# A transformer block with table-coded weights: look-ups twice as wide, down's first weights parked in DRAM, and the last weights copied one unit earlier

## The chip, the core and the metric

One core of a Trainium2 chip runs the kernel in one launch. The metric is the device time of that launch in microseconds (us), as the median of several runs. A separate execution was recorded by the hardware profiler; all views of the profile come from that one execution. Engines are named as in the profile: PE (TensorE, matmuls), PEld (its weight loads), DVE (VectorE), ACT (ScalarE), POOL (GpSimd, which here only issues DMAs), SP (SyncE, which only issues DMAs). "L783" is line 783 of the kernel.

## The reference

The block is attention across the embedding axis, and then a gated feed-forward layer whose weights are 4-bit indices into a table of 16 numbers:

```python
x = x + attn(_layernorm(x), Wq, Wk, Wv, Wo)     # x: 2 x 2048 x 512, float32
w = lut[idx]                                    # lut: 16 numbers; idx: int32, 0 to 15
gate = einsum('bsh,oh->bso', y, lut[gate_idx])  # y = _layernorm(x); gate_idx: 1376 x 512
up   = einsum('bsh,oh->bso', y, lut[up_idx])    # up_idx: 1376 x 512
h    = silu(gate) * up
x    = x + einsum('bso,ho->bsh', h, lut[down_idx])   # down_idx: 512 x 1376
```

## The kernel before, in words

**Stages.** The 4096 rows are taken as 8 chunks c of 512 rows, four blocks j of 128 in each. First come the Gram matrices of the normalised rows (`gram`, L458), then products of 512 x 512 matrices in Strassen's manner (`square`, L662) with the softmax among them, then y, the attention's result (`y_product`, L779), and the second norm. Then follow the gate/up units (`GateUp`, L1013), the rows of the last 96 hidden columns (`LastRows`, L1232) and the down product in 32 units (`Down`, L1413).

**Blocks of hidden columns.** 1376 is 10 blocks f of 128 and one of 96 (`NFT` = 11). A gate/up unit (f, p) makes block f for the pair p of chunks. All products are Strassen products: sums of operands are made on DVE, products are added up in PSUM, and parts are copied out by ACT or added by DVE. From f = 2 on two units are joined into a second level; such a unit has a role: 0 and 1 for even f (p even, odd), 2 and 3 for odd f. Units of role 3 are short.

**Order.** Each engine's instructions run in the order in which the program writes them, and the order is written by hand. A unit runs in stages (`Line.run`, L1179), and after each stage `between` (L1311) is called. It may write a load, some waiting sums, or a little of the look-ups: `pump(us)` (L407) adds `us` to an account and calls `step` (L398) until the account is used up. `step` writes the next piece of work, whose cost in the planner's microseconds is what the generator yields. `pace` sets how much a stage gives: 0.85, 1.4, 1.0 and 0.6 for roles 0 to 3.

**Look-ups.** `looked_up` (L381) runs through `jobs` (L376). A job (`Job`, L246) turns up to 128 x 512 indices into weights. `fetch` loads them from DRAM by POOL's queue, `cast` makes 16-bit copies on ACT (L259), and `ops` writes 19 DVE instructions: three masks (L271, L272, L277), the lowest bit spread into a mask (L275), and a tree of eight selections between two table entries ("leaves", L285) with seven predicated copies (L297). The eighth leaf is the 16th of the 19 instructions, and three copies follow it. Gate and up of a block are two jobs; each of down's 11 blocks is one. Index tiles have two buffers: job i + 2 is fetched when job i has been written, and job i + 1 is cast in the middle of job i. A job's `gate` keeps it from starting before its destination is free: `passed` and `ended` count the f whose last unit has been written, or has had its fourth a-product written in the following unit.

**Weights.** Gate weights lie in `wg` and up weights in `wu`, three buffers each. The sums of both (`of_both`, L345) are put off until an older f has ended. Down's first six blocks stay in SBUF from their look-up to the end, in `wd` (L119, 12 KB of each partition); the others are looked up during the down product, into `wd2`.

**The end of the units.** After the last unit (9, 3) the program writes what is left of the look-ups, opens new pools, asks SP for three loads of h (L1371), and has ACT copy the last block's gate and up weights side by side into one tile (L1250, L1251). Then 16 groups of 16 matmuls follow (L1285), each in one of four PSUM banks in turn; ACT and DVE empty a group into `hrow`. Between the groups DVE makes further sums of the last weights and of down's first blocks (`down_sums`, L1346).

## Time and profile before

| what | value |
|---|---|
| median of 3 runs | 1066.43 us (1066.21 to 1067.09) |
| the profiled execution's own time | 1067.22 us |
| its span from first to last instruction | 1065.4 us |
| granted TensorE clock | full |
| moved by DMA | 189 MB, 177 GB/s over the span |

The span by stage (busy us of each engine in each stretch, from the span's start):

| stage | stretch | PE | DVE | ACT |
|---|---|---|---|---|
| Gram matrices | 7 to 77 | 69.4 | 57.2 | 40.1 |
| matrix products, softmax | 77 to 165 | 87.7 | 70.3 | 31.9 |
| y and second norm | 165 to 275 | 110.0 | 96.7 | 50.6 |
| units f = 0, 1 | 275 to 383 | 108.0 | 85.7 | 38.2 |
| units f = 2 to 9 | 383 to 750 | 365.7 | 313.0 | 155.5 |
| last rows | 750 to 793 | 42.3 | 18.9 | 6.5 |
| down, first half | 793 to 935 | 142.0 | 122.3 | 42.4 |
| down, second half | 935 to 1062 | 127.0 | 70.2 | 17.9 |

How to read the profile's lines. A line of the costliest groups or of instructions by line has: line, engine, operation, tiles (written<-read, buffer numbers left out), shape, count | busy us, mean ns of one | idle us of the engine before them and what ended it. A line of the waits has: who waited, for whom, us in total, times, longest. A timeline line has: start, duration, engine, line, operation, tiles, count, and in brackets the engine's idle time before. Matmuls overlap, and their ends are modelled, so lateness shows best in the steps from start to start.

### The profile page before, as it was taken

How to read it: one execution, taken by the hardware profiler on the slowest of the kernel's cores; microseconds unless marked ns; L12 is line 12 of the kernel's file. 1: busy time of each engine (PE TensorE's matmuls, PEld its weight loads, DVE VectorE, ACT ScalarE, POOL GpSimd, SP SyncE). 2: the span in 40 equal slices, each digit the busy share in tenths (PEclk: the TensorE clock that was granted, in tenths of full speed). 3: DMA queues.
4: the chain of work that ended last, by engine and by line, in shares of the span. 5: the costliest groups of instructions: out<-in, count | busy, mean ns of one | idle time of the engine just before them, and what ended most of it. 6: DMA issues, size and time to landing. Idle time of an engine off the chain costs nothing. (4 is left out here: it accounts for less than half of the span.)

```text
span 1065.4 us, 11592 instructions
## 1 busy us (share of the span) xinstructions
PE 1056.6 (99%) x3554; PEld 660.7 (62%) x3554; DVE 837.1 (79%) x1842; ACT 385.2 (36%) x741; POOL 105.7 (10%) x160
## 2 busy tenths in 40 slices
PE   8999999999999999999999999999999999999998
PEld 5668887444444444444444444444898888888887
DVE  7878778889985889899699999964549998656554
ACT  4652532455532234444443444443223222211111
POOL 0000000011110220230041032013000000000000
PEclk9999999999999999999999999999999999999999
DMA  8750314598561366795596679569436675666773
GB/s 345 236 169 11 86 28 99 119 237 222 158 178 50 128 228 197 172 220 183 185 207 198 208 174 225 178 192 195 150 114 230 198 228 177 203 192 211 222 227 119
DMA packets 127710, 189.07 MB, mean 177 GB/s; under 512 B 18832, under 2 KB 59024, under 8 KB 126752
## 3 DMA queue, kind: packets, MB, share of 16 engines
q1 hardware_dynamic: 74528, 100.17, 29.6%
q0 software_dynamic: 15776, 39.92, 17.4%
q10 hardware_dynamic: 37344, 48.24, 13.9%
q8 instruction: 28, 0.46, 0.2%
q14 instruction: 34, 0.28, 0.1%
HBM read 108.60 MB, written 79.69 MB: 177 GB/s over the span
## 5 line engine op out<-in xcount | busy, mean ns | idle before, releaser
L783 PE MATMUL y<-m,nT 128*128 128x512 f32 x256 | 110.2, 592 | 0.0
L783 PEld LDWEIGHTS y<-m,nT 128*128 128x128 f32 x256 | 48.6, 190 | 60.4 <-issue 57.4
L1008 PE MATMUL a_g<-xT_a,s 128*128 128x512 f32 x160 | 75.5, 594 | 0.0
L1008 PE MATMUL a_g<-xb,wg 128*128 128x512 f32 x160 | 75.4, 593 | 0.0
L1008 PE MATMUL c_g<-xb,wu 128*128 128x512 f32 x160 | 75.2, 592 | 0.0
L1008 PE MATMUL a_d<-dT,hs_a 128*128 128x256 f32 x288 | 72.6, 379 | 0.0
L467 PE MATMUL gp<-xn_a 128*128 128x128 f32 (+3 forms) x256 | 70.1, 434 | 1.8 <-DVE xn_a L184 1.5
L467 PEld LDWEIGHTS gp<-xn_a 128*128 128x128 f32 x256 | 43.9, 190 | 28.6 <-issue 15.1
L1008 PEld LDWEIGHTS a_d<-dT,hs_a 128*128 128x128 f32 x288 | 54.5, 189 | 7.7
L297 DVE COPY_PREDICATED wd<-b_wd,wd 128x512 f32<-128x512 int16 (+1 forms) x77 | 56.3, 732 | 1.3
L1008 PE MATMUL a_g<-xT_sq,s 128*128 128x512 f32 x120 | 56.7, 595 | 0.0
L1473 ACT COPY p_d<-a_d 128x256 f32<-128x256 f32 x32 | 11.9, 372 | 120.2 <-PE a_d L1008 120.2
L1008 PEld LDWEIGHTS a_g<-xb,wg 128*128 128x128 f32 x160 | 30.2, 190 | 39.0 <-issue 32.5
L1008 PEld LDWEIGHTS a_g<-xT_a,s 128*128 128x128 f32 x160 | 30.1, 190 | 38.9 <-issue 36.4
L1008 PEld LDWEIGHTS c_g<-xb,wu 128*128 128x128 f32 x160 | 30.4, 190 | 38.3 <-issue 38.0
L143 DVE TENSOR_TENSOR r<-r,p_d 128x256 f32<-128x256 f32 x64 | 26.9, 420 | 28.0 <-ACT p_d L1473 17.4
L285 DVE TENSOR_SCALAR wd<-idx_wd,lut_x,lut_sb 128x512 int32<-128x512 int32 (+1 forms) x88 | 45.9, 539 | 0.0
L1063 ACT COPY u<-a_g 128x512 f32<-128x512 f32 x40 | 23.4, 586 | 61.9 <-PE a_g L1008 59.5
L143 DVE TENSOR_TENSOR u<-c_g,u 128x512 f32<-128x512 f32 x40 | 27.5, 688 | 21.8 <-PE c_g L1008 15.5
L1285 PE MATMUL rows<-last,xb 128*128 128x192 f32 x256 | 41.9, 326 | 1.6 <-ACT last L1251 1.6
L1285 PEld LDWEIGHTS rows<-last,xb 128*128 128x128 f32 x256 | 41.6, 190 | 2.5 <-ACT last L1251 2.5
L143 DVE TENSOR_TENSOR r<-r,a_d 128x256 f32<-128x256 f32 x64 | 26.6, 416 | 20.9 <-PE a_d L1008 20.9
(345 smaller groups left out, 2207.1 us busy)
## 6 DMA issues: line engine op xcount, KB each, us to landing
hd<-h SPq DMA_DIRECT2D x80, 256.0 KB, 3.3
h<-hd SPq DMA_DIRECT2D x40, 512.0 KB, 5.9
nl<-nd SPq DMA_DIRECT2D x32, 256.0 KB, 5.6
xnd<-xn_f ACTq DMA_DIRECT2D x16, 512.0 KB, 5.9
fl<-xnd POOLq DMA_DIRECT2D x32, 256.0 KB, 6.7
xn_back<-xnd SPq DMA_DIRECT2D x32, 256.0 KB, 3.9
rd<-r SPq DMA_DIRECT2D x32, 256.0 KB, 3.0
r<-rd SPq DMA_DIRECT2D x32, 256.0 KB, 4.3
```

The source lines that it names most:

```text
L143: nc.vector.tensor_tensor(dest, a, b, ALU.add)
L285: vec.tensor_scalar(dest.bitcast(I32), idx, lut_x[:rows, k : k + 1], lut_i[:rows, at : at + 1], ALU.bitwise_and, ALU.bitwise_xor,)
L297: vec.copy_predicated(dest, masks[level - 1], t)
L467: nc.tensor.matmul(gp[b][i][:, i * P :], xn[:, i, j % 2, :], xn[:, i:, j % 2, :], start=c % CPB == 0 and j == 0, stop=c % CPB == CPB - 1 a ...
L783: nc.tensor.matmul(ys[k], nTs[k][:, i, :], m[:, i, :], start=(i == 0), stop=(i == KB - 1))
L1008: nc.tensor.matmul(ps, lhsT, rhs, start=first and i == 0, stop=i == len(pairs) - 1, skip_group_check=not first,)
L1063: nc.scalar.copy(self.u2, self.a)
L1285: nc.tensor.matmul(ps[:, jj, :], x[:, j * P : (j + 1) * P], w, start=i == 0, stop=i == len(pairs) - 1,)
L1473: nc.scalar.copy(p1, self.a)
```

## The change

A job now covers two tables' worth of columns: gate and up of one block together (`pair_job`), or two neighbouring blocks of down, 1024 columns in one instruction. There are 17 jobs in place of 33. There is one index tile, twice as wide; the next job is fetched right after the eighth leaf of the running one (`LEAVES` = 15) and cast after the running one's last instruction, with 0.9 of planner's cost for the cast. All planner's costs of the look-ups are new. A pair's gate is that of the former up job. Gate and up weights of a block share one tile `w` with three buffers. The first fetch, of two transfers, stays on SP; the second, formerly also on SP after the loads of x, goes to POOL.

Down's first six blocks are looked up two at a time into one staging buffer `wds`, stored by SP into `wdd` in DRAM, and loaded again by SP at the end of the units, behind the loads of h, into the rooms `sq1` (four blocks) and `a3` (two).

Before unit (9, 3) the program writes what is left of the last pair's look-up, and ACT's two copies of the last weights.

```diff
-    wd = wdp.tile([P, K1, E], F32, tag="wd", name="wd")
+    wdd = dram.tile([P, K1, E], F32, tag="wdd", name="wdd")
...
         def fetch(self, queue=nc.gpsimd):
-            self.idx = gub.tile([P, 512], I32, tag="idx", name=f"idx_{self.name}", bufs=2)[
-                : self.rows, : self.cols
-            ]
-            self.load(queue, self.idx)
+            t = gub.tile([P, 2, 512], I32, tag="idx", name=f"idx_{self.name}", bufs=1)
+            self.idx = self.part(t)
+            for i, of in enumerate(self.loads):
+                queue.dma_start(self.idx[:, i, :], of)
 
         def cast(self):
-            self.b3 = self.bits("b3", 2)
-            nc.scalar.copy(self.b3, self.idx)
+            self.b1 = self.bits("b1")
+            nc.scalar.copy(self.b1, self.idx)
...
-            vec.tensor_scalar(b1, b3, 2, None, ALU.bitwise_and)
-            vec.tensor_scalar(b2, b3, 4, None, ALU.bitwise_and)
-            yield 0.2 + 0.54 * f
+            b2, b3 = self.bits("b2"), self.bits("b3")
+            vec.tensor_scalar(b2, b1, 4, None, ALU.bitwise_and)
+            yield 0.15 + 0.24 * f
+            vec.tensor_scalar(b3, b1, 8, None, ALU.bitwise_and)
+            yield 0.15 + 0.24 * f
+            vec.tensor_scalar(b1, b1, 2, None, ALU.bitwise_and)
+            yield 0.15 + 0.24 * f
 
             vec.tensor_scalar(idx, idx, 31, 31, ALU.logical_shift_left, ALU.arith_shift_right)
-            yield 0.1 + 0.55 * f
-            vec.tensor_scalar(b3, b3, 8, None, ALU.bitwise_and)
-            yield 0.1 + 0.27 * f
+            yield 0.15 + 0.48 * f
...
-                    yield 0.2 + 0.55 * f
+                    yield 0.25 + 0.48 * f
...
                 vec.copy_predicated(dest, masks[level - 1], t)
-                yield 0.1 + 1.17 * f
+                yield 0.18 + 0.96 * f
...
+        def dest():
+            if i < K1:
+                t = wgu.tile([P, 2, E], F32, tag="wds", name=f"wd_{i}", bufs=1)
+            else:
+                t = wd2[0][:, i - K1 : i - K1 + k, :]
+            made.append(t[:rows, :k, :])
+            return made[0]
+
+        def after():
+            if i < K1:
+                nc.sync.dma_start(wdd[:, i : i + k, :], made[0])
+            yield 0.1
...
+    jobs = [pair_job(0), pair_job(1), down_job(0), down_job(2)]
+    for f in range(2, NFT - 1):
+        jobs.append(pair_job(f))
+        if f == 7:
+            jobs.append(down_job(4))
+    jobs += [pair_job(NFT - 1), *(down_job(i) for i in range(K1, NFT, 2))]
...
             if i == 0:
                 job.cast()
+                yield 0.9
             for k, cost in enumerate(job.ops()):
                 yield cost
-                if k == 9 and i + 1 < len(jobs):
-                    jobs[i + 1].cast()
-            if i + 2 < len(jobs):
-                jobs[i + 2].fetch()
+                if k == LEAVES and i + 1 < len(jobs):
+                    jobs[i + 1].fetch()
+            if i + 1 < len(jobs):
+                jobs[i + 1].cast()
+                yield 0.9
+
+    LEAVES = 15
...
-    jobs[1].fetch(nc.sync)
...
+        def copied(self):
+            f, r = NFT - 1, LAST
+            nc.scalar.copy(self.w[:, :, :r], gw[f])
+            nc.scalar.copy(self.w[:, :, r:], uw[f])
...
+        if (f, p) == (NFT - 2, NPR - 1):
+            while uw.get(NFT - 1) is None:
+                step()
+            last_rows = LastRows()
+            last_rows.copied()
         u = GateUp(f, p)
...
-    last_rows = LastRows()
+    for q, (tag, n) in enumerate((("sq1", 4), ("a3", 2))):
+        t = room(tag, f"wd_{tag}")[:, :n, :]
+        nc.sync.dma_start(t, wdd[:, 4 * q : 4 * q + n, :])
+        wd1 += [t[:, i, :] for i in range(n)]
```

More of the change, by code (lines that the diff above doesn't have):

```diff
@@ L109, in tile_attn_ffn @@
     small = ctx.enter_context(tc.tile_pool(name="small", bufs=3))
-    wdp = ctx.enter_context(tc.tile_pool(name="wdp", bufs=1))
     dram = ctx.enter_context(tc.tile_pool(name="dram", bufs=1, space=DRAM))
@@ L246, in tile_attn_ffn, with __init__, part @@
     class Job:
-        def __init__(self, name, rows, cols, load, dest, after, gate):
+        def __init__(self, name, rows, cols, loads, dest, after, gate):
             self.name, self.rows, self.cols = name, rows, cols
-            self.load, self.dest, self.after, self.gate = load, dest, after, gate
+            self.loads, self.dest, self.after, self.gate = loads, dest, after, gate
+        def part(self, t):
+            return t[: self.rows, : len(self.loads), : self.cols]
         def fetch(self, queue=nc.gpsimd):
-            self.idx = gub.tile([P, 512], I32, tag="idx", name=f"idx_{self.name}", bufs=2)[
-                : self.rows, : self.cols
-            ]
-            self.load(queue, self.idx)
+            t = gub.tile([P, 2, 512], I32, tag="idx", name=f"idx_{self.name}", bufs=1)
+            self.idx = self.part(t)
+            for i, of in enumerate(self.loads):
+                queue.dma_start(self.idx[:, i, :], of)
@@ L257, in cast, with bits @@
         def cast(self):
-            self.b3 = self.bits("b3", 2)
-            nc.scalar.copy(self.b3, self.idx)
-        def bits(self, tag, bufs):
-            t = gub.tile([P, 512], I16, tag=tag, name=f"{tag}_{self.name}", bufs=bufs)
-            return t[: self.rows, : self.cols]
+            self.b1 = self.bits("b1")
+            nc.scalar.copy(self.b1, self.idx)
+        def bits(self, tag):
+            t = gub.tile([P, 2, 512], I16, tag="b", name=f"{tag}_{self.name}", bufs=3)
+            return self.part(t)
@@ L265, in ops @@
         def ops(self):
-            rows, f, idx, b3 = self.rows, self.cols / 1024, self.idx, self.b3
+            rows, f, idx, b1 = self.rows, len(self.loads) * self.cols / 1024, self.idx, self.b1
             vec = nc.vector
             w = self.dest()
-            b1, b2 = self.bits("b1", 1), self.bits("b2", 1)
-            vec.tensor_scalar(b1, b3, 2, None, ALU.bitwise_and)
-            vec.tensor_scalar(b2, b3, 4, None, ALU.bitwise_and)
-            yield 0.2 + 0.54 * f
+            b2, b3 = self.bits("b2"), self.bits("b3")
@@ L292, in pick @@
                 half = 1 << (level - 1)
-                t = gub.tile(
-                    [P, 512], F32, tag="pick", name=f"{self.name}_{level}_{at}", bufs=3
-                )[:rows, : self.cols]
+                t = self.part(gub.tile(
+                    [P, 2, 512], F32, tag="pick", name=f"{self.name}_{level}_{at}", bufs=3
+                ))
                 yield from pick(level - 1, at + half, t)
                 vec.copy_predicated(dest, masks[level - 1], t)
-                yield 0.1 + 1.17 * f
+                yield 0.18 + 0.96 * f
             yield from pick(4, 0, w)
@@ L307, in tile_attn_ffn, with pair_job @@
     ended = [0]
-    def gate_job(f):
+    def pair_job(f):
         f0, rows = FT[f]
         n = KB * rows
-        def load(queue, idx):
-            queue.dma_start(idx, gate_idx[:, KB * f0 : KB * f0 + n])
+        made = []
         def dest():
-            t = wgu.tile([P, KB, P], F32, tag="wg", name=f"wg_{f}", bufs=3)
-            gw[f] = t.rearrange("p k r -> p (k r)")[:, :n]
-            return gw[f]
+            made.append(wgu.tile([P, 2, KB * P], F32, tag="w", name=f"w_{f}", bufs=3)[:, :, :n])
+            return made[0]
         def after():
-            gw[f] = gw[f].rearrange("p (k r) -> p k r", k=KB)
-            yield 0.1
-        return Job(f"g{f}", P, n, load, dest, after, lambda: f < 3 + passed[0])
-    def up_job(f):
-        f0, rows = FT[f]
-        n = KB * rows
-        up = []
-        def load(queue, idx):
-            queue.dma_start(idx, up_idx[:, KB * f0 : KB * f0 + n])
-        def dest():
-            t = wgu.tile([P, KB, P], F32, tag="wu", name=f"wu_{f}", bufs=3)
-            up.append(t.rearrange("p k r -> p (k r)")[:, :n])
-            return up[0]
-        def after():
-            uw[f] = up[0].rearrange("p (k r) -> p k r", k=KB)
+            for to, i in ((gw, 0), (uw, 1)):
+                to[f] = made[0][:, i, :].rearrange("p (k r) -> p k r", k=KB)
             if f < NFT - 1:
@@ L356, in of_both @@
             gu[f] = {"11": a11, "12": a12, "S3": a21, "22": a22, "S1": s1, "S2": s2, "S4": s4}
-        return Job(f"u{f}", P, n, load, dest, after, lambda: f < 3 + ended[0])
+        loads = [idx[:, KB * f0 : KB * f0 + n] for idx in (gate_idx, up_idx)]
+        return Job(f"w{f}", P, n, loads, dest, after, lambda: f < 3 + ended[0])
     def down_job(i):
         f0, rows = FT[i]
-        return Job(
-            f"wd{i}", rows, E, lambda queue, idx: queue.dma_start(idx, down_idx[f0 : f0 + rows, :]),
-            lambda: wd_block(i)[:rows], lambda: iter(()), lambda: i < K1 or wd2,
-        )
+        k = 2 if i + 1 < NFT else 1
+        made = []
+        def dest():
[4 more added lines that the diff above has]
+            made.append(t[:rows, :k, :])
+            return made[0]
+        def after():
+            if i < K1:
+                nc.sync.dma_start(wdd[:, i : i + k, :], made[0])
+            yield 0.1
+        loads = [down_idx[f0 + P * q : f0 + P * q + rows, :] for q in range(k)]
+        return Job(f"wd{i}", rows, E, loads, dest, after, lambda: i < K1 or wd2)
     wd2 = []
+    wd1 = []
     def wd_block(i):
-        return wd[:, i, :] if i < K1 else wd2[0][:, i - K1, :]
-    jobs = [job(f) for f in range(2) for job in (gate_job, up_job)]
-    jobs += [down_job(i) for i in range(4)]
-    for f in range(2, NFT - 1, 2):
-        jobs += [gate_job(f), up_job(f), gate_job(f + 1), up_job(f + 1)]
-        jobs += [down_job(i) for i in {6: (4,), 8: (5,)}.get(f, ())]
-    jobs += [gate_job(NFT - 1), up_job(NFT - 1), *(down_job(i) for i in range(K1, NFT))]
-    assert len(jobs) == 3 * NFT
+        return wd1[i] if i < K1 else wd2[0][:, i - K1, :]
+    jobs = [pair_job(0), pair_job(1), down_job(0), down_job(2)]
[4 more added lines that the diff above has]
+    jobs += [pair_job(NFT - 1), *(down_job(i) for i in range(K1, NFT, 2))]
+    assert len(jobs) == NFT + (NFT + 1) // 2
     def looked_up():
@@ L925, in ready @@
         def ready(self, f):
-            return f in gu if self is of_d else f in gw and len(gw[f].shape) == 3 and f in uw
+            return f in gu if self is of_d else f in uw
         def sums_left(self, f):
@@ L1238, in __init__ @@
         def __init__(self):
-            s = [wgu.tile([P, 3, 2, P], F32, tag="s", name=f"last_{i}", bufs=2) for i in range(2)]
-            flat = [
-                t.rearrange("p a b c -> p (a b c)").rearrange("p (k r) -> p k r", k=KB) for t in s
-            ]
-            self.w, self.v = flat
-            t = last_pool.tile([P, KB, 2 * LAST], F32, tag="last", name="last_2")
-            self.u = t
+            self.w, self.v = (
+                wgu.tile([P, 3, 2, P], F32, tag="s", name=f"last_{i}", bufs=2)
+                .rearrange("p a b c -> p (a b c)").rearrange("p (k r) -> p k r", k=KB)
+                for i in range(2)
+            )
+        def copied(self):
+            f, r = NFT - 1, LAST
+            nc.scalar.copy(self.w[:, :, :r], gw[f])
+            nc.scalar.copy(self.w[:, :, r:], uw[f])
         def weights(self):
-            f, r = NFT - 1, LAST
-            w, v, u = self.w, self.v, self.u
-            nc.scalar.copy(w[:, :, :r], gw[f])
-            nc.scalar.copy(w[:, :, r:], uw[f])
+            w, v = self.w, self.v
+            self.u = u = last_pool.tile([P, KB, 2 * LAST], F32, tag="last", name="last_2")
             minus = nc.vector.tensor_scalar_mul
@@ L1573, in tile_attn_ffn @@
                     in_place.append(last)
-    while uw.get(NFT - 1) is None:
-        step()
     assert not todo and next(lookup, None) is None
```

## The prediction

> **What bounds the kernel now.** I read the page's totals, then who TensorE (PE) waited for, then the timeline around the late matmuls, then the costs of the instructions that the change touches.

> ```profile
> PE 1056.6 (99%) x3554; PEld 660.7 (62%) x3554; DVE 837.1 (79%) x1842; ACT 385.2 (36%) x741; POOL 105.7 (10%) x160
> ```

> PE is busy for all but 8.8 us. VectorE (DVE), whose work the change cuts most, is not the bound on average: less DVE work is worth only what it takes out of PE's waits. The waits of PE:

> ```profile
> PE rows L1285 <- ACT last L1251: 1.6, 1, 1.6
> PE gp L467 <- DVE xn_a L184: 1.5, 1, 1.5
> PE idle L447 <- POOL ident masks.py:199: 1.4, 1, 1.4
> PE ea_s L620 <- ACT a L641: 0.3, 1, 0.3
> PE z_g L1008 <- DVE lc L140: 0.2, 1, 0.2
> PE z_g L1008 <- ACT r_c L958: 0.2, 1, 0.2
> ```

> The largest is the copy of the last weights, which the change moves. A small lateness hides in the modelled end of a matmul, so I also went through all matmul starts of the timeline and set each against the usual step of its shape (0.429 us for 512 columns, 0.215 for 256, 0.162 for the 192 of rows). The lateness adds up to 9.9 us: 3.8 in the first 25 us, 1.4 from 50 to 150 us, 2.9 in the gate/up units from 383 to 750, 1.8 at the first rows. Everything that this change could win lies in the last three, some 6 us. Of the 2.9, eight times 0.085 (0.7) follow the copy of u in the short units (odd f, odd p), which is untouched.

> **The copies ahead.** Today:

> ```profile
> 747.07 1.96 PE L1008 MATMUL a_g<-xT_sq,s 128*128 128x512 f32 x4
> 749.70 0.49 ACT L1250 COPY last<-wg 128x384 f32<-128x384 f32 x1
> 750.10 0.51 ACT L1251 COPY last<-wu 128x384 f32<-128x384 f32 x1
> 750.66 41.87 PE L1285 MATMUL rows<-last,xb 128*128 128x192 f32 x256 [1.63 <-ACT last L1251]
> ```

> Four matmuls from 747.07 at 0.43 end their turn at 748.79; rows start at 750.66, so 1.87 us late. ACT reaches the copies late because two silus (748.64, 749.18) wait for other things first. Moved ahead of unit (9,3), the copies meet an ACT that stands idle from 740.90 to 742.98 before its copy of p; they take 0.91 of these 2.08 us. Without this cover they would delay that copy by up to 0.91, and the next matmul on its bank comes two stages (3.4 us) later. Price there 0. The first four rows' groups need nothing but these copies, and the sums u and v that DVE makes are first used in the fifth group, 10 us on. **Gain 1.87** (at least the 1.6 idle). The forced steps ahead of (9,3) issue nothing: its look-ups ended at 705.6 today.

> **Look-ups of 1024 columns.** Rows of 512 and 384 columns give each instruction's fixed part and slope:

> ```profile
> L297 DVE COPY_PREDICATED wd<-b_wd,wd 128x512 f32<-128x512 int16 x70 | 51.2, 732 | 1.3
> L297 DVE COPY_PREDICATED u<-b_u,u 128x384 f32<-128x384 int16 x4 | 2.4, 588 | 0.1
> L285 DVE TENSOR_SCALAR wd<-idx_wd,lut_x,lut_sb 128x512 int32<-128x512 int32 x80 | 41.6, 539 | 0.0
> L285 DVE TENSOR_SCALAR g<-idx_g,lut_x,lut_sb 128x384 int32<-128x384 int32 x7 | 3.1, 472 | 0.0
> L259 ACT CAST b_wd<-idx_wd 128x512 int16<-128x512 int32 x10 | 6.2, 618 | 0.6 <-ACT xn_f L239 0.6
> L259 ACT CAST b_g<-idx_g 128x384 int16<-128x384 int32 x1 | 0.5, 512 | 0.0
> ```

> A copy costs 144 ns more for 128 more columns, so 732 + 4 x 144 = 1308 at 1024 (twice 732 at most); a leaf 539 + 4 x 67 = 0.81; a cast 618 + 4 x 106 = 1.04; the masks go from 0.284 to 0.42, the sign mask from 0.417 to 0.68 (rows of 512 and 384 again). One look-up today is 3 x 0.284 + 0.417 + 8 x 0.539 + 7 x 0.732 = 10.7; two are 21.4. One of 1024 is 3 x 0.42 + 0.68 + 8 x 0.81 + 7 x 1.308 = 17.6. Sixteen such pairs save 3.8 each: some **61 us of DVE**, 7% of its work. The planner's costs fall alike (19.6 to 16.6 a pair, 0.9 of it for the cast), so a look-up ends sooner rather than DVE being emptier beside it. On the path this buys one thing for sure: at 394.57 a z_g matmul is 0.46 late (0.355, then 0.104) for the sums lc, which wait for up 3, ended at 390.6. Gate and up 3 took 45 us; at 16.6/19.6 that is 38, less about 4 because the joint gate waits for a unit's a4 rather than for an earlier mark. That is 3 us sooner, where 0.5 is wanted: **gain 0.46**.

> **Longer lumps.** Today a cast can make PE late:

> ```profile
> 579.40 0.62 ACT L259 CAST b_g<-idx_g 128x512 int16<-128x512 int32 x1
> 579.92 0.59 ACT L958 COPY r_c<-z_g 128x512 f32<-128x512 f32 x1
> 580.56 1.12 PE L1008 MATMUL z_g<-T_c_in,lc 128*128 128x512 f32 x2 [0.15 <-ACT r_c L958]
> ```

> The matmul is 0.42 late with its successor, and 0.25 at 672.20 in the same way: two of some seventeen casts of this stretch cost 0.67. Afterwards nine casts stand there, each 0.43 longer. If one meets this place it costs 0.42 + 0.43, so +0.2 against today; none would be -0.67, all nine +7.0. I take **+0.2**, by the share today. On DVE, a1 of the unit after a short one waits for the last a4's addition: 0.28 late at 565.55, 0.25 at 657.37, with one look-up instruction in that chain. A copy is 0.58 longer; four or five short units have look-ups beside them, so between -0.53 and +2.9. **+0.2**, because look-ups now cover fewer of these units, but with larger pieces.

> **One index buffer.** The fetch of the next indices now waits for the last leaf (it reads the only buffer), and its cast follows three copies later on ACT, in front of PSUM copies. Today fetch and cast stand a whole job apart, and no cast waits for a DMA. POOL issues 0.3 us after the leaf (358.4 to 358.69, and alike elsewhere), 0.56 for the first transfer, and from its issue a 256 KB fetch lands after 2.7 to 6.2, mostly 3.8, in the gate/up stretch: the pair is there 0.86 + 3.8 = 4.7 us after the leaf. From the last leaf to the start of the third copy took 2.4 us (median of those jobs) at 1.37 of planner's cost; now the cost is 2.28, so 4.0, and the third copy's 1.24 must be paid before the cast is written: 5.4 on average, anything from 3 to 8. ACT waits in perhaps a third of nine cases, about 1 us each; before its copies in the last unit it is idle 2.08, 1.18 and 1.09, so the first microsecond is free. Bounds 0 and, with the slowest landing (7.1) against the earliest cast (3) each time, 9 x 3 = 27. By the typical rows **+0.3**. [...]

> POOL's fetch itself is 0.54 to 0.58 right behind a leaf. [...]

> **Down's blocks through DRAM.** Three 512 KB stores go on SP's queue. Each waits for a DVE copy written just before it, and what SP holds behind it (loads of nd, stores of hd) is written later, so waits for later DVE work anyway. The second look-up into the one staging buffer waits for the first store: about 6 us to land (the 512 KB row of 5.9) against 2.8 of planner's cost, 6 us at 1.6 per 3.44 us block; a microsecond at most on DVE, where normalised rows are turned a block ahead. At the end 1.5 MB come back behind the three loads of h, which landed at 755.9, 757.3 and 758.6. At the 322 GB/s of 755 to 760 the rest needs 4.7 more: 763.3. The first sum, today at 759.4, would run at 757.5 and wait some 4.5 us for the first 1 MB; behind it on DVE stand the rows' products. Rows use four PSUM banks of 2.6 us each, so PE feels it only from about 769. **0**, with 6 us of cover; without that each further microsecond is one lost. The first indices' second 256 KB ahead of x4 costs under 1 us in a queue whose x4 landed at 19.9 and is used from 33 on (a chunk takes PE 8.6 from 7.25): 0.

> **Sum.** -1.87 - 0.46 + 0.2 + 0.2 + 0.3 = -1.6. The profiled execution's 1067.22 becomes 1065.6; it stands 0.8 above the median of the runs, so the median becomes 1066.43 - 1.6 = **1064.8**. A measurement can't tell less than about 0.2% (2.1 us) from no change: "the same" is 1064.3 to 1068.6.

> **Rivals.**
> 1. **All new lumps are hidden and old ones go** (36%). The lateness at 499.0 (0.25), 565, 580, 657 and 672 (1.2) vanishes too: -1.87 - 0.46 - 1.45 = -3.8, 1062.7; with half of it 1063.4. For: fewer casts and fewer units with look-ups. Against: each piece is 1.6 to 1.8 times as long.
> 2. **ACT waits for the index pair** (17%), slower. If the second transfer lands like the one issued at 385.0 (6.2 us), it is there 7.1 after the leaf, and ACT stands 1.7 at the cast; less 1 us of slack that is 0.7 on PE, nine times: 6.3 - 2.33 + 0.4 = +4.4, 1070.8. It decides from a landing of 6.9 on (0.45 each time undoes the gains and 2.1 more). For: a single buffer, two transfers that share the engines. Against: the median 3.8.
> 3. **The DRAM round trip is late** (3%): weights that land at 774 instead of 763 would cost 5 us, 1068 to 1070. Against: nothing else in that stretch moves much (0.12 of DMA after 760).

> My forecast, the gain of the copies mostly kept and little else, has 44%, from 1064.3 to 1066.5. So faster 36%, the same 44%, slower 20%. The range runs from 1062.8 (rival 1 nearly whole) to 1069.5 (half of rival 2).

> **What would show it.** Right: rows start about 0.43 us after the last a_g with no wait on ACT; DVE busy near 776; casts of 1.04, copies of 1.31. Wrong: casts on ACT, or masks on DVE, that wait for DMA idx; z_g or x_g late behind a cast; rows waiting for dT; gate/up lateness well away from 2.9.

## The result, and the profile after

The changed kernel takes **1080.72 us** (median of 4 runs, 1078.18 to 1082.72) beside 1066.74 for the kernel before in the same comparison: a ratio of 1.013 with a 95% interval of [1.0108, 1.0152]. It is slower by 14 us, outside the range. The profiled execution took 1078.18 us, its span is 1076.4 us (before 1065.4), and its mean granted clock is 0.998 (before full).

First the parts of the page that answer to those of before: the totals, and the two groups of look-up instructions that cost most. In a group the columns are busy us, mean ns of one, and idle us before them.

```profile
PE 1060.0 (98%) x3554; PEld 661.2 (61%) x3554; DVE 800.1 (74%) x1538; ACT 382.2 (36%) x725; POOL 106.5 (10%) x160
...
L302 DVE COPY_PREDICATED w<-b_w,w 128x1024 f32<-128x1024 int16 (+1 forms) x77 | 98.6, 1280 | 1.4
...
L290 DVE TENSOR_SCALAR w<-idx_w,lut_x,lut_sb 128x1024 int32<-128x1024 int32 (+1 forms) x88 | 67.7, 793 | 0.3
```

DVE has 304 instructions fewer. Their durations add up to 881 us where they added up to 942: the 61 us of the prediction are gone from DVE. Apart by shape, a copy of 1024 columns takes 1.306 us and a leaf 0.805. PE is nevertheless 11 us longer under way. What it waited for (who, for whom: us in total, times, longest):

```profile
PE a_g L1012 <- DVE h L142: 6.2, 4, 2.3
PE a_g L1012 <- ACT b_g L1047: 1.9, 1, 1.9
PE a_g L1012 <- ACT p L1047: 1.8, 3, 1.0
...
PE a_g L1012 <- ACT u L1067: 1.0, 1, 1.0
```

The rows' wait for ACT's copies and the z_g wait for lc no longer stand there. In their place PE waits for DVE and ACT inside the gate/up units. Set against the usual steps, the lateness of all matmul starts is now 20.8 us, 9.9 before. The span less this lateness is 1055.5 us before and 1055.6 after, and within 0.2 us of that in every experiment: lateness accounts for the whole of the difference. By its places, in us:

| place in the changed kernel | lateness against before |
|---|---|
| behind DVE in short units: matmuls at 456.80, 553.11, 573.80, 647.92, with 1.8 us of half-speed steps after the first | +9.0 |
| behind an ACT copy of p that stands behind a silu, which waits for DVE: 449.90, 546.21 | +1.35 |
| behind a cast that waited for its indices: 473.35, 568.99, 666.33, 700.26 | +5.0 |
| copies ahead, lc at 394, the old casts and short units (499, 565, 580, 657, 672) | -1.87, -0.46, -1.45 |
| start, softmax and rest | about -0.7 |

**The first loss: DVE in a short unit.** The timeline (start, us, engine, line, operation, tiles; in brackets idle before and its releaser) around the first of them:

```profile
452.58 1.96 PE L1012 MATMUL a_g<-xT_a,s 128*128 128x512 f32 x4
...
453.49 0.69 DVE L1146 TENSOR_TENSOR h<-h,u 128x512 f32<-128x512 f32 x1
...
454.10 1.30 DVE L302 COPY_PREDICATED w<-b_w,w 128x1024 f32<-128x1024 int16 x1
455.29 0.68 DVE L142 TENSOR_TENSOR y<-w_g,y 128x512 f32<-128x512 f32 x1
456.06 0.69 DVE L142 TENSOR_TENSOR h<-a_g,y 128x512 f32<-128x512 f32 x1
...
456.80 3.66 PE L1012 MATMUL a_g<-xb,w 128*128 128x512 f32 x4 [2.26 <-DVE h L142]
```

The same place of before, where the four matmuls at 454.99 are on time:

```profile
452.07 0.69 DVE L1142 TENSOR_TENSOR h<-h,u 128x512 f32<-128x512 f32 x1
...
452.68 0.73 DVE L297 COPY_PREDICATED wg<-b_g,g 128x512 f32<-128x512 int16 x1
...
453.19 1.96 PE L1008 MATMUL a_g<-xT_a,s 128*128 128x512 f32 x4
453.30 0.68 DVE L143 TENSOR_TENSOR y<-w_g,y 128x512 f32<-128x512 f32 x1
...
454.07 0.69 DVE L143 TENSOR_TENSOR h<-a_g,y 128x512 f32<-128x512 f32 x1
...
454.99 1.88 PE L1008 MATMUL a_g<-xb,wg 128*128 128x512 f32 x4
```

DVE hardly rests here. The matmul at 456.80 needs the bank that `h<-a_g,y` empties. Measured from the start of the four matmuls before it, DVE came to `h<-h,u` at +0.91 us, and in the same unit of before at -1.12: it was 2.0 us in arrears already, and then a copy 0.57 longer stood in between. Where the arrears come from shows when the look-up's DVE instructions are added up over the 12 us that end where the matmul was due (1.8 us after the start of the four before it): 8.1 us at 457 and 553, and 6.2 in the kernel before. A window of fixed length lets other work of a late DVE slip out of it, so the same is better counted in program order: from the four sums s with which this stretch begins to `h<-a_g,y`, DVE has the same twelve other instructions in both kernels, and between them there are 9.1 us of look-up at 457 and 553 and 5.8 in the kernel before. These places were given 3.3 us more. At 648 it is 6.5, too little to explain 1.8 us of lateness. There DVE came late to the stretch: at 634.47 it had waited 2.19 us for ACT's copy `h<-w_g`, which stood behind a cast, a silu and four copies that ACT had done without a rest since 630.44, when its own wait of 5.67 us for DVE ended.

Why the stretch was given more can be read, though no run tests it alone. In before the gate half of a pair may start earlier than the up half (435.97 here), and in the 8 us before the sums s DVE is idle for 1.4 us. In after the joint gate keeps the whole pair back until 442.77, right behind the sums, and DVE is idle for 5.4 of these 8 us; meanwhile `pump` lets the unused account grow up to twice a stage's `us` plus 1.0, which the short unit then has to take.

The same place by windows (us of the window; busy us and count of each engine; granted clock; DMA share; GB/s):

```profile
core 0: us, PE busy (x) PEld busy (x) DVE busy (x) ACT busy (x) POOL busy (x), PEclk, DMA share, GB/s
452.50:456.80 4.30, 2.04 (x5) 0.68 (x4) 4.07 (x7) 0.02 (x2) 0.88 (x1) 1.00 0.99 207
456.80:460.70 3.90, 3.90 (x5) 1.70 (x6) 3.76 (x5) 1.28 (x3) 0.57 (x1) 0.56 0.48 155
...
553.10:557.00 3.90, 3.89 (x9) 1.82 (x10) 3.76 (x5) 2.25 (x4) 0.57 (x1) 1.00 0.45 159
```

DVE is busy for 4.07 of 4.30 us. And after PE's idle 2.26 us the granted clock is 0.56: the matmuls from 456.80 on start 1.01, 0.85, 0.85 and 0.77 us apart instead of 0.43, which costs 1.8 us more. After the equal stall at 553.11 the clock stays 1.00 (see the last section).

**The second loss: ACT stands at casts.** Its waits for index DMAs; before there were none:

```profile
ACT b_wd L263 <- DMA idx_wd<-in_down_idx_dram: 8.3, 3, 6.4
ACT b_w L263 <- DMA idx_w<-in_up_idx_dram: 5.3, 4, 1.8
```

The longest, in the timeline:

```profile
691.23 0.67 DVE L290 TENSOR_SCALAR w<-idx_w,lut_x,lut_sb 128x768 int32<-128x768 int32 x1
...
692.19 1.06 POOL L259 DMA_DIRECT2D idx_wd<-in_down_idx_dram  x2 [0.17 <-issue]
...
698.68 1.04 ACT L263 CAST b_wd<-idx_wd 128x1024 int16<-128x1024 int32 x1 [6.39 <-DMA idx_wd<-in_down_idx_dram]
...
699.63 0.58 ACT L1047 COPY b_g<-a_g 128x512 f32<-128x512 f32 x1
...
700.26 1.98 PE L1012 MATMUL a_g<-xT_a,s 128*128 128x512 f32 x4 [1.91 <-ACT b_g L1047]
```

The last leaf ends at 691.90, the fetch is issued 0.3 us later and lands 6.4 us after its issue. ACT had come to the cast at 692.29, and PE's bank waits behind it. Over the eight casts from 383 to 760 us the pair landed 5.2 to 9.2 us after the leaf (median 6.7), and ACT was there after 3.6 to 7.7, this one after 0.4.

### The profile page after: what moved, and what is told of

Its sections match the earlier page's. It is cut to its first block, busy times and chain, and to the rows that moved or that the text cites. A ratio compares the mean times of both kernels' runs of the same rounds, so it can differ in the third digit from the quotient of the medians.

```text
span 1076.4 us, 11315 instructions
## 1 busy us (share of the span) xinstructions
PE 1060.0 (98%) x3554; PEld 661.2 (61%) x3554; DVE 800.1 (74%) x1538; ACT 382.2 (36%) x725; POOL 106.5 (10%) x160
## 5 line engine op out<-in xcount | busy, mean ns | idle before, releaser
L302 DVE COPY_PREDICATED w<-b_w,w 128x1024 f32<-128x1024 int16 (+1 forms) x77 | 98.6, 1280 | 1.4
L1012 PE MATMUL a_g<-xb,w 128*128 128x512 f32 x160 | 77.3, 606 | 6.2 <-DVE h L142 6.2
L1012 PE MATMUL c_g<-xb,w 128*128 128x512 f32 x160 | 75.2, 592 | 0.0
L290 DVE TENSOR_SCALAR w<-idx_w,lut_x,lut_sb 128x1024 int32<-128x1024 int32 (+1 forms) x88 | 67.7, 793 | 0.3
L1012 PEld LDWEIGHTS a_g<-xb,w 128*128 128x128 f32 x160 | 30.6, 193 | 46.5 <-issue 35.2
L1012 PEld LDWEIGHTS c_g<-xb,w 128*128 128x128 f32 x160 | 30.4, 190 | 38.3 <-issue 38.0
L302 DVE COPY_PREDICATED wd<-b_wd,wd 128x1024 f32<-128x1024 int16 (+1 forms) x42 | 50.8, 1210 | 0.4
```

The lines of the kernel that those rows point to most:

```text
L290: vec.tensor_scalar(dest.bitcast(I32), idx, lut_x[:rows, k : k + 1], lut_i[:rows, at : at + 1], ALU.bitwise_and, ALU.bitwise_xor,)
L302: vec.copy_predicated(dest, masks[level - 1], t)
L1012: nc.tensor.matmul(ps, lhsT, rhs, start=first and i == 0, stop=i == len(pairs) - 1, skip_group_check=not first,)
```

## The experiments

"Lateness" is that of the profiled run, summed as above.

| kernel | median us (runs) | ratio to before, 95% | lateness us |
|---|---|---|---|
| before | 1066.2 to 1066.7 in the comparisons | 1 | 9.9 |
| after | 1080.72 (4) | 1.013 [1.0108, 1.0152] | 20.8 |
| e1 cast at the gate | 1070.54 (4) | 1.0043 [1.0028, 1.0058] | 12.7 |
| e2 fewer look-ups in short units | 1074.17 (4) | 1.0076 [1.0059, 1.0093] | 16.3 |
| e3 both | 1080.47 (4) | 1.0136 [1.0121, 1.0151] | 24.5 |
| e4 only the copies ahead | 1065.29 (10) | 0.9987 [0.9978, 0.9997] | 8.0 |
| e5 = e1, down's blocks 4, 5 last | 1071.12 (4) | 1.0047 [1.0032, 1.0062] | 14.6 |
| e6 = e5, fewer look-ups in short units | 1067.49 (10) | 1.0012 [1.0002, 1.0021] | 10.5 |
| e7 = e5, copies of 512 columns | 1069.93 (5) | 1.0035 [1.0021, 1.0049] | 12.3 |
| e8 = e5, prices as measured | 1068.64 (7) | 1.0024 [1.0013, 1.0035] | 11.1 |
| e9 narrow look-ups, one index buffer | 1087.50 (4) | 1.0199 [1.0173, 1.0226] | 32.4 |
| e10 = all mends | 1063.79 (9) | 0.9975 [0.9965, 0.9985] | 6.5 |
| e11 fetch on SP | 1081.62 (4) | 1.0144 [1.0113, 1.0174] | 26.3 |
| e12 = e10, cast behind the job before | 1066.02 (10) | 0.999 [0.9981, 1.0] | 9.8 |

**e1: is it the cast's place?** A job is cast when its gate opens, instead of right behind the job before; where the gate is open already, 2.0 of the account is spent first, so that the fetch has time.

```diff
+            waited = i == 0
             ...
-            if i == 0:
-                job.cast()
-                yield 0.9
+            if not waited:
+                yield 2.0
+            job.cast()
+            yield 0.9
...
-            if i + 1 < len(jobs):
-                jobs[i + 1].cast()
-                yield 0.9
```

> The changed kernel, but a job is cast when its gate opens (2.0 of planner's cost later where the gate stands open) and no longer right after the job before it. Theory (ACT stands at casts for the index DMA, and apart from that DVE's longer pieces delay the short units): the waits of ACT for DMA idx near 471, 567, 605, 665 and 698 us go, PE's lateness falls by the 5 us that follow such casts, the 9 to 10 us behind DVE in the short units stay; about 1075. Rival, the fetch alone is to blame: 1065 to 1067. Rival, only the length of DVE's pieces: 1079 to 1081, unchanged.

Measured: 10.2 us less than after, more than expected. PE's waits in e1:

```profile
PE a_g L1012 <- DVE h L142: 3.2, 2, 1.6
...
PE z_g L1012 <- DVE lc L139: 1.1, 1, 1.1
```

ACT's waits for indices are gone, and with them all matmuls late behind a cast. Also gone are the half-speed steps (the mean clock is 1.000 for 0.998 in after), the late p copies and the third late short unit; two short units are still 1.89 late each. The edit does two things, it moves the cast and spends account: the look-up in the two short units fell from 9.1 to 7.8 us in program order. So not all of the 10 us is ACT's wait; matmuls late behind a cast had cost 5.0. New is that the sums lc of block 9 come late (673.75, 1.39).

**e2 and e3: less DVE work in short units.** The pace of role 3 goes from 0.6 to 0.3, alone (e2) and on top of e1 (e3).

```diff
-        pace[0] = {0: 0.85, 1: 1.4, 2: 1.0, 3: 0.6}.get(u.role, 1.07)
+        pace[0] = {0: 0.85, 1: 1.4, 2: 1.0, 3: 0.3}.get(u.role, 1.07)
```

> The changed kernel with half the look-up work written into units of role 3 (pace 0.3 in place of 0.6). Theory: the late a_g matmuls behind DVE's addition of h (2.4 us at 456.8, 2.4 at 553.1, 1.7 at 647.9) shrink to under 0.5 each, and with them the half-speed matmuls after the first of them; ACT's waits for idx stay; about 1071 to 1073. Rival, the fetch alone is to blame: 1079 to 1081.

> Both edits. Theory: nothing else is wrong with the change, so PE's lateness from 383 us on falls below 3 us and the time to 1063 to 1066, the gain of the copies kept. Rival, something else (the DRAM round trip, longer pieces everywhere): stays above 1069.

In e2 the short units at 457 and 553 went from 2.42 late to 1.24, that at 648 from 1.71 to nothing: 6.5 us of median, to a time above the expected 1071 to 1073. ACT's waits for indices did not stay, as had been expected: of the casts in this stretch two still waited, 0.3 and 2.9 us, and no matmul was late behind them. With the lighter pace ACT comes to six of the eight casts 7.2 to 11.0 us after the leaf, so this edit too takes away a part of both losses. But less look-up per unit means that the weights are ready later, and block 9's sums became the bound. e3 missed its expectation by 14 us for the same reason. PE's waits in e3:

```profile
PE z_g L1012 <- DVE lc L139: 11.0, 1, 11.0
```

One wait of 11 us for block 9, and about 3 us of half-speed steps behind it (clock 0.50 from 682.4 to 686.0 us). A third limit had come up that neither theory had: the pair of block 9 has a date, and down's blocks 4 and 5 stand in front of it.

**e4: the copies alone, on the kernel before.** The block `if (f, p) == (NFT - 2, NPR - 1)` of the change is added to the kernel before, with `LastRows.copied`.

> The kernel before with the two copies of the last weights ahead of unit (9,3) and nothing else. By the prediction's term 1.87 us less than before: 1064.5 to 1065.2, rows starting 0.43 us after the last a_g. Rival, the copies collide with ACT's work in unit (9,3): no gain, 1066.4.

1065.29 beside 1066.47: -1.2 us in the median, and 1.9 in the spans and the lateness of the profiled runs. The rows start on time, as the first term of the sum has it. The median lies just above the 1064.5 to 1065.2 that were expected; the interval, -0.3 to -2.3 us, holds the 1.87.

**e5 and e6: the date of block 9.** Down's blocks 4 and 5 are looked up after the last pair; e6 has pace 0.3 for role 3 as well.

```diff
-        if f == 7:
-            jobs.append(down_job(4))
-    jobs += [pair_job(NFT - 1), *(down_job(i) for i in range(K1, NFT, 2))]
+    jobs += [pair_job(NFT - 1), down_job(4), *(down_job(i) for i in range(K1, NFT, 2))]
```

> Casts at the gate, and down's blocks 4 and 5 looked up after pair 10, no longer between pairs 7 and 8. Theory: the wait of z_g for the sums lc at (8,1) (1.4 us in the run with casts at the gate, 4 and 11 us in the two with lighter short units) is pair 9 finished too late, since blocks 4 and 5 stand ahead of it; it goes here: 1.4 us less than with casts at the gate alone, 1069 to 1069.5. What stays is the 1.9 us behind DVE in each of two short units. Rival, that wait has another cause: 1070.5.

> As the run with blocks 4 and 5 last, and half the look-up work in units of role 3. Theory: the short units' lateness behind DVE falls from 1.9 to 0.6 to 1.0 each; pair 9 is just in time: 1066.5 to 1067.5. Rival, pair 9 is late again: a wait of z_g for lc at (8,1), above 1069.

e5's wait for lc is gone, but the time stays: now a third short unit is 1.97 late, beside the first two with 1.90. The look-ups of block 9 moved into it. That missed the expectation and says that work taken from one place in this stretch comes back in the next short unit, unless the pace there falls. With it (e6) the lateness is 0.72, 1.07 and 0.82, and the time fell where it was expected.

**e7 and e8: length of a piece, or its price?** Both on e5. e7 makes each copy in two of 512 columns at half the planner's cost each; e8 leaves the pieces and sets their price to what they take.

```diff
-                vec.copy_predicated(dest, masks[level - 1], t)
-                yield 0.18 + 0.96 * f
+                for q in range(len(self.loads)):
+                    vec.copy_predicated(dest[:, q, :], masks[level - 1][:, q, :], t[:, q, :])
+                    yield 0.09 + 0.48 * f
```

```diff
-                    yield 0.25 + 0.48 * f
+                    yield 0.25 + 0.56 * f
...
-                yield 0.18 + 0.96 * f
+                yield 0.18 + 1.13 * f
```

> As the run with blocks 4 and 5 last, but each predicated copy of 1024 columns is written as two of 512, each with half the planner's cost; leaves, masks and casts stay 1024 wide. DVE has some 0.15 us more to do per copy. Theory (the length of the pieces delays the chain in the short units): lateness at 457 and 550 falls from 1.9 to 0.3 to 0.8 each, 1066.5 to 1068. Rival (the amount of work in the short units, not its grain): 1.9 or more each, 1069 to 1071.

> As the run with blocks 4 and 5 last, with planner's costs as measured: 1.31 a copy in place of 1.14, 0.81 a leaf in place of 0.73. Same instructions, only where they are written moves. Theory (grain): lateness in the short units moves with the phase but doesn't go, 1.0 to 2.5 each, 1068 to 1070. Rival (the pieces are underpriced, so the planner overfills the short units): lateness below 0.6 each, 1066.5 to 1067.5.

PE's waits for DVE's h in e5, and the two waits in the units of e8:

```profile
PE a_g L1010 <- DVE h L142: 5.3, 4, 1.7
```

```profile
PE z_g L1010 <- DVE lc L139: 1.8, 1, 1.8
...
PE a_g L1010 <- DVE h L142: 1.3, 3, 0.4
```

Neither expectation was met whole. e7 has the time of its rival (1069 to 1071), with less lateness than that expected; e8 has the time of its theory (1068 to 1070), but a new wait of 2 us is in it, and its short units lie near the rival's 0.6. A late short unit costs 1.9 in e5, 1.37 with short pieces and 0.72 with true prices. The look-up in the short unit's stretch, in program order as above, can be set against the lateness behind it in all kernels of the study (the units at about 457 and 550):

| kernel | look-up in the stretch, us | lateness of each unit, with the step behind it, us |
|---|---|---|
| e10 | 5.7 | 0 |
| before, e4, e9 | 5.8 | 0 |
| e12 | 6.5 | 0.60 |
| e8 | 6.5 | 0.72 |
| e3, e6 | 6.5 | 0.72 and 1.07 |
| e7 | 7.4 | 1.37 |
| e2 | 7.8 | 1.34 |
| e1, e5 | 7.8 | 1.9 |
| after, e11 | 9.1 | 2.5 |

So the lateness goes with the amount that the units are given. Pieces of 1024 columns make neither unit late in e10, and e7's gain over e5 comes with 0.4 us less look-up: apart from the amount, no effect of a piece's length shows above the spread of about half a us between kernels of the same amount. The change's prices are too low by 11% for a pair (15.7 without the cast, for 17.6), and by 13% for a copy (1.14 for 1.31); but those of before were too low as well, by 8% (19.6 for 21.4) and 6%. The step in price is small, therefore: true prices mend the amount, but they need not be what had raised it. How the price and the later opening of the joint gate share in that is open. With true prices the look-ups as a whole are slower, and block 3's sums come 2.06 late at 396; the pace of the first units (f = 0, 1) has to make up for that.

**e9: the single index buffer at the old width.** The kernel before, with one index tile, the fetch behind the last leaf, and the cast behind the last copy; the second job's early fetch on SP is gone as well.

```diff
-            self.idx = gub.tile([P, 512], I32, tag="idx", name=f"idx_{self.name}", bufs=2)[
+            self.idx = gub.tile([P, 512], I32, tag="idx", name=f"idx_{self.name}", bufs=1)[
...
-                if k == 9 and i + 1 < len(jobs):
-                    jobs[i + 1].cast()
-            if i + 2 < len(jobs):
-                jobs[i + 2].fetch()
+                if k == 14 and i + 1 < len(jobs):
+                    jobs[i + 1].fetch()
+            if i + 1 < len(jobs):
+                jobs[i + 1].cast()
```

> The kernel before, look-ups of 512 columns, but with one index buffer: the next job is fetched behind the last leaf and cast behind the last copy, as in the changed kernel. Theory (the late cast costs by itself, whatever the width): a fetch lands some 4 us after the leaf, the cast comes after three copies of 2.05 planner's cost, some 3.5 us; ACT waits for DMA idx at many of the seventeen casts of the gate/up units, 1068 to 1074. Rival (only wide look-ups suffer, since two transfers must land): 1066 to 1067.

It lost 21 us, more than any expectation. Who ACT waited for in e9:

```profile
ACT b_g L259 <- DMA idx_g<-in_gate_idx_dram: 24.0, 8, 4.7
ACT b_wd L259 <- DMA idx_wd<-in_down_idx_dram: 14.0, 5, 8.7
```

With four casts of up indices (9.9), 17 casts wait 48 us in all. So this order of fetch and cast costs time by itself, without a long piece or a new price; with twice the jobs, and 2.05 instead of 3.42 of account between fetch and cast, it costs more than in the change. The two short units of the table above are on time in e9.

**e11: is POOL's queue the cause?** After, with the fetches on SP.

```diff
-        def fetch(self, queue=nc.gpsimd):
+        def fetch(self, queue=nc.sync):
```

> The changed kernel with the index fetches on SP's queue in place of POOL's, nothing else. Theory: in the short units POOL is crowded with accumulating transfers, so the pair lands 8 us after the leaf there; on SP it should land after 4 to 6, and ACT waits at casts for under half as long: 1075 to 1079, the lateness behind DVE stays. Rival (the landing is slow whatever the queue, since the DMA engines are shared, or SP waits for stores of h): 1080 to 1083.

The time is no better, and the casts still wait, 12 us in all:

```profile
ACT b_w L263 <- DMA idx_w<-in_up_idx_dram: 7.3, 3, 3.8
ACT b_wd L263 <- DMA idx_wd<-in_down_idx_dram: 4.9, 1, 4.9
```

A pair issued on SP at 466.70 and 467.19 landed at 473.9 and 476.4, up to 9.7 us; it had stood behind a store of h for 1.8 us after its leaf. Another was issued right behind its leaf, at 699.48, and landed at 704.15; ACT had come to its cast at 699.37. Over the eight casts from 383 to 760 us the second transfer lands 3.5 to 9.7 us after the first one's issue, with a median of 4.7, beside 4.9 to 8.9 and 6.4 in after. So by the median SP's pairs land sooner, but two slow pairs (9.7 and 8.0) and one early ACT are enough for the waits: POOL's queue alone isn't their cause. What made these two pairs slow was not measured.

**e10 and e12: everything mended, and the cast put back.** e10 is e5 with e8's prices, pace 0.3 for role 3 and 1.3 instead of 1.07 for f = 0, 1. e12 is e10 with the cast behind the job before, as in the change.

> The changed kernel with all mends: casts at the gate, blocks 4 and 5 last, costs as measured, half the look-up work in role 3, and 1.3 in place of 1.07 per stage in units f = 0, 1, so that pair 3 is done by (2,1). Theory: lateness in the short units below 0.4 each, no wait for lc, no wait for idx; 1063.5 to 1065.5, about the copies' gain. Rival (something of the change costs besides): 1067 or more.

> As the run with all mends (1063.8), but each cast again right behind the job before it, as in the changed kernel. Theory (the waits of ACT for the index DMA cost by themselves, with DVE's part of the loss mended): ACT waits for DMA idx at four or more casts, PE late by 4 to 7 us behind them: 1068 to 1072. Rival (the waits hurt only together with DVE's lateness in the short units): 1064 to 1066.

e10 is the fastest kernel of the study, 1063.79 us, 2.6 below before. PE is busy for 1055.0 of its span of 1062.2 us. Of its waits inside the units one is left, 0.70 late at 564.96. e12 lost 2.2 of this: it lies at the upper end of its rival's 1064 to 1066, not at the theory's 1068 to 1072, and the ACT waits of e12 say why:

```profile
ACT b_wd L263 <- DMA idx_wd<-in_down_idx_dram: 2.1, 2, 1.4
```

No cast of gate or up waits any more. The pair still lands 5.1 to 7.1 us after the leaf, but with true prices and light short units ACT comes to the cast after 6.4 to 12.2. So the wait for the indices was not fixed by the order alone: the same pace that overfilled DVE also brought the cast forward. What e12 loses shows as some 0.6 us in each of three short units, without a wait for indices. They hold one leaf more of look-up (6.5 us for 5.7): in e10 the cast's price of 0.9 is paid there, when the gate opens, in e12 earlier. The rest of the profiled run's lateness over e10 (2.1 of 3.3 us) lies in its first 25 us; that run stands 1.2 us above e12's median.

## Why the prediction was wrong

**The copies ahead: right.** The rows start on time in after:

```profile
759.68 1.96 PE L1012 MATMUL a_g<-xT_sq,s 128*128 128x512 f32 x4
...
761.48 2.76 PE L1290 MATMUL rows<-last,xb 128*128 128x192 f32 x16
```

Four matmuls of 0.43 from 759.68 end their turn at 761.40; the 1.87 us are gone, and e4 shows them alone.

**The look-ups' cost: right.** Copy 1.306 us (said 1.308), leaf 0.805 (0.81), cast 1.04; DVE's 61 us; lc of block 3 no longer late.

**Longer lumps: the failed step.** On DVE the sum held +0.2 where 10.3 was lost (9.0 directly, 1.35 through silu and p), even above the step's upper end of 2.9 and that of 7.0 for the casts. Two things failed in "+0.2, because look-ups now cover fewer of these units, but with larger pieces". It priced only one longer piece in one chain, while two of the units were given 9.1 us of look-up in place of 5.8, and made PE 2.5 us late each: e8 took 1.2 of the 1.9 us of lateness that e5 still had away by prices alone. The new price of a copy stood in the diff, 0.18 + 0.96, and the prediction itself put the copy at 1.31; I set the prices only against the old ones ("The planner's costs fall alike"), and never added up what a short unit holds. It also took the joint gate only for a delay of some 4 us of pair 3, not for work that moves into the short units. And fewer short units with look-ups did not help, since each one that is left is full. The stall at 456.80 had also a second price that no row of before showed, 1.8 us of half-speed steps.

**One index buffer: too small a size.** +0.3 was taken and 5.0 lost at four casts. The cast was put at 5.4 us after the leaf "on average", and six of the eight came within 5.2 to 7.7. The landing failed: 4.7 was said and the median is 6.7, since the 3.8 of one transfer was used for the second of two, and two pairs in short units, with one of POOL's own accumulating transfers between their two issues, took 8.9 us (issues at 462.81 and 465.36, landed at 471.69) and 8.3 (559.02 and 560.12, landed at 567.33) where the other six took 4.9 to 6.5. And ACT does not come to the cast when DVE has done the third copy: the order in which the program writes is only the order within ACT, which at 692.29 had nothing else before it.

**The rivals.** Rival 2, ACT waiting for the pair, was the right side and nearly the right price for its own mechanism: 6.3 us on PE by landings of 7.1, with 5.0 measured at a median of 6.7. Its 1070.8 lacked DVE's part. Rival 1 was right that the old lateness of 1.45 vanishes; it went with ten times as much that came.

**The DRAM round trip: right.** DVE waits for the weights from DRAM, PE does not; the prediction said some 4.5 us. DVE's waits in after:

```profile
DVE dT L139 <- DMA wd_sq<-wdd: 3.9, 1, 3.9
```

## What to carry to other kernels

When a hand-made planner spreads work under a busy engine, compare each price in the diff with the measured duration of the piece, and look at the fullest stage of the covering engine, not at its average: 61 us of DVE work saved over the span bought nothing, while a late DVE in a few short units, two of them with some 3 us too much, cost 10. When a double buffer becomes a single one, set the slowest landing in the crowded stretches against the earliest time at which the reading engine can come to its instruction by its own queue. Work taken out of a full stage must be followed to where it is late next (e3, e5).

## What the runs showed of the hardware

Some stalls of PE had a second price, half clock behind them: behind the stall of 2.26 us in after, the matmuls of 512 columns from 456.80 on start 1.01, 0.85, 0.85 and 0.77 us apart instead of 0.43. The trace records when the granted clock changes, and within each of the 14 profiles all changes lie whole multiples of 3.41 us apart (in after 450.56, 3.41 and 617.81 us, which is 132, 1 and 181 of them; in before 1061.55 us, which is 311). These multiples, counted from the recorded changes, are the grid below. In after, half clock lasts from 456.8 to 460.2, one interval of that grid (clock 0.50), and costs 1.8 us. Behind the 3.9 us of e2 it is also one interval (clock 0.57 from 676 to 680 us). In the 11.0 us of e3 it begins during the stall and ends 5.7 us after it, which costs about 3 us (clock 0.66 from 671 to 682.4 us, 0.50 to 686, 0.72 to 690); in e9, behind a lateness of 3.87, it is two intervals (clock 0.94 from 873 to 877.7 us, 0.50 to 882, 0.76 to 886), and some 15 steps of 256 columns last 0.43 instead of 0.215.

Stalls of equal length, with half clock behind the one and full clock behind the other, differ when PE's idle time is cut at the borders of this grid (the ends of matmuls are modelled):

| stall of PE, by its end | idle us | of it in single intervals, us | clock behind it |
|---|---|---|---|
| after, 456.80 | 2.26 | 2.25 and 0.01 | half |
| after, 553.11 | 2.26 | 1.51 and 0.75 | full |
| e11, 459.27 | 2.26 | 0.65 and 1.60 | full |
| e11, 559.54 | 2.27 | 2.27 | half |
| e9, 244.47 | 2.53 | 0.28 and 2.25 | half |
| e8, 396.46 | 1.79 | 1.79 | full |
